# A decoder in one launch: how the second attention hands out VectorE work between its maxima

## The chip, the core and the metric

The kernel runs on one core of one Trainium2 chip. The metric is the device time of one execution in microseconds (us). It is taken as a median of several runs of the same program; beside them one execution is profiled, which gives the rows and the trace that this document quotes. Five engines work from queues of their own: TensorE (PE; its weight loads are listed as PEld), VectorE (DVE), ScalarE (ACT), GpSimd (POOL) and SyncE (SP, which here only issues DMAs). Each engine takes its instructions in the order in which the program emits them, so the order of emission is the schedule.

## The reference

Four residual blocks work on `x` of 4 batches x 512 tokens x 256 features, all in float32:

```python
x = x + L0_xattn(layernorm(x), ctx)   # 8 heads of 4, softmax(q k^T * scale) v, then Wo
x = x + L0_ffn(layernorm(x))          # 8 experts, the best 2 for each token, at most 640 tokens for an expert
x = x + L1_xattn(layernorm(x), ctx)   # 16 heads of 16
x = x + L1_ffn(layernorm(x))          # 15 experts, the best 3 for each token, and a shared expert for all tokens
```

In the last block the router is a softmax over 15 logits for each token; the weights of the three best are normed to a sum of one. An expert computes `fc2(gelu(g) * xh * mult) + b2` with `xh, g = fc1(x) + b1`. The shared expert does the same with twice the width for every token.

## The kernel before

The kernel goes through these stages in order: first attention, the pairs of tiles of the first expert block, second attention, the pairs of tiles of the second expert block, and the sum of the results. Tokens of the expert blocks are written ("put") into a table in DRAM, `xs`, sorted by expert, by indirect DMAs of GpSimd, three for each of the four tiles of 128 tokens in a batch; the experts then read pairs of tiles from it.

**The steps of an attention.** `attention(L, ...)` is a software pipeline written out by hand, counted in steps `t`. A unit is a batch, a group of 8 heads and one half of the group; the second attention has N = 16 units (4 batches, 2 groups, 2 halves) of 8 steps each, so 128 steps. In each step are emitted

- two score products and two row maxima (`maximum`, L669 and L674; VectorE reduces 128x512 scores from PSUM to `negmax`), for the unit that is LEAD = 11 steps ahead,
- two transposed score products and two exponentials (`exponential`, L693 and L698, ScalarE),
- in every other step four products of exponentials and values (`weigh`, L708).

The scores live in a pool of six PSUM banks (`ps_sc`); a step takes four of them, and a bank comes free when its maximum or its exponential has been taken.

**Tasks.** Everything else of the attention with a due time is a task with an earliest and a latest step, given a step of its own by `choose` and `meets`: `helper` (L682, L684, the maxima turned and added to q), `project` (L646 to L661: q or k for a group; two masked copies, one on ScalarE at L659 and one on VectorE at L661, save that k of batches 1 and 2 has both on ScalarE), `values`, `turn`, `rest` (L723 to L739, the division), `turn_back`, `output` (L765, L770).

**Generators.** What has no due time is a generator that yields before each piece of its work. `normalize(b)` adds the results of the first expert block (`combine`, two adds of 128x1024, L1192), takes the mean and variance of the rows (`layer_norm`, L192 to L212), writes the normed rows on ScalarE (L591), and adds the output bias to `x` (L596). It is started 26 steps ahead of the batch's first maximum. `route(f, b, ...)` starts when the second half of the batch's `output` is emitted: again `layer_norm`, four copies of the normed rows into `rows` (L246, ScalarE; one buffer for batches 0 to 2, so batch b+1 has to wait until the puts of batch b have read it), two transposes (L259), logits (L269), some thirty small VectorE instructions for softmax, the best three, counts and places (L280 to L356), the puts (L365, L367) and the transposed weights `combT` (L382, L385). After batch 3 follows `listing` (L401 to L445), which names the pairs that are to be computed.

At the end of each step every living generator runs one piece (two, if it routes batch 1, and two for all once t > 8N). A piece marked TensorE waits for a step without a task.

**The end of the attention.** Two steps after the last unit, `some_shared` begins: one piece a step of the shared expert for batches 0, 1 and 2 in turn, as long as `listing` is not done (`while more[0] < B - 1 and not listed`). What is left of batches 0 to 2 is computed right after the attention, behind the issue of the first three experts' weights and rows (`fetch1`); batch 3's is computed at the very end, and so is what surrounds it:

```python
        for p in range(3):
            fetch1(p)
        for b in more[:-1]:
            for step in (shared_expert, biases):
```

Of the kernel before, what the change touches and what calls it, by code (L numbers as in the profile page):

```python
# [22 lines left out]
P = 128  # L23
# [50 lines left out]
def decoder_kernel(ctx: ExitStack, tc: tile.TileContext, a: dict, out: bass.AP):  # L74
# [106 lines left out]
    V, PEP = "beside", "TensorE"  # L181

    def layer_norm(i, apply, twice=False):
# [4 lines left out]
        for k in range(n):  # L188
            if k % 2 == 0:
                yield V  # L190
# [14 lines left out]
        for step in range(3):  # L205
            if step == 1:
                yield V
# [4 lines left out]
        nc.vector.scalar_tensor_tensor(shift, mv[:, :, 0], -1.0, r, ALU.mult, ALU.mult)  # L212
        for k in range(n):
            yield V
            apply(k, r[:, k : k + 1], shift[:, k : k + 1])
# [24 lines left out]
    def route(f, b, pool, bank):  # L240

        n, K, first = f.n, f.k, f is ffn0
        rows = f.new_rows(b)

        def apply(k, scale, shift):
            nc.scalar.activation(  # L246
# [4 lines left out]
        yield from layer_norm(x[b], apply, twice=first)  # L251
# [3 lines left out]
        for c in range(DC):  # L255
# [4 lines left out]
            if first:  # L260
                scaled(xT[:, c, :], pt, c)
            else:
                (nc.vector.tensor_copy if c == 0 else nc.scalar.copy)(xT[:, c, :], pt)
        logits = pool.tile([P, TB, n], F32, name="logits", tag="logits")
# [34 lines left out]
        )  # L299
        picked = pool.tile([P, TB, n], F32, name="picked", tag="picked")  # L300
        nc.vector.tensor_reduce(picked, chosen.rearrange("p t k e -> p t e k"), AX.X, ALU.add)

        past = pool.tile([P, TB + 1, n], F32, name="past", tag="past", bufs=2)
# [18 lines left out]
        if not first:  # L322
# [6 lines left out]

            by = pool.tile([P, TB, K, n], F32, name="by", tag="by")  # L330
# [30 lines left out]
        for k in range(TB):  # L361
            for _ in range(K):
                yield V
# [14 lines left out]
        if not first:  # L378
# [6 lines left out]
            nc.scalar.copy(combT[:, b * S : (b + 1) * S], pc[: n + 1, :])  # L385
        f.done.add(b)
# [149 lines left out]

    LEAD = 11

    def attention(L, begin, behind, others=None):
# [43 lines left out]
        going = []  # L583

        def normalize(b):
# [7 lines left out]
            yield from layer_norm(x[b], apply)  # L593
            if not shared:
                yield V
                nc.vector.tensor_tensor(x[b], x[b], W["bo"].unsqueeze(1).to_broadcast([P, TB, D]), ALU.add)  # L596
# [7 lines left out]
        def turn(b, c):  # L604
            xn, t = xnT[b]
            pt = ahead([P, S], 0 if b else -LEAD)
# [34 lines left out]
        def project(b, g, n, at=0):  # L641
# [8 lines left out]
            for s in range(2):  # L650
# [7 lines left out]
                elif s == 0 or (n == "k" and 0 < b < B - 1):  # L658
# [126 lines left out]
        def task(lo, hi, f, *needs):  # L785
            tasks.append((lo, hi, f, needs))
# [3 lines left out]
        for n, u in enumerate(units):  # L790
            task(8 * n - 3, 8 * n - 1, lambda u=u: helper(u))
            if not shared or u[2] == 1:
                rests[u] = task(8 * n + 10, 8 * n + (12 if shared and u[0] == 1 else 15), lambda u=u: rest.pop(u)())
        for b in range(B):
            at = 8 * U * b - LEAD
            starts[at - 26] = [lambda b=b: normalize(b)]
# [670 lines left out]
```

## Time and profile before

| | |
|---|---|
| median of 3 runs | 1244.99 us (1244.24 to 1246.53) |
| the profiled execution | 1261.71 us; span of its instructions 1259.7 us, mean granted TensorE clock 0.970 |
| busy: PE, DVE, ACT, POOL | 1183.7, 588.3, 473.2, 192.1 us |
| second attention, first maximum to last exponential | 624.1 to 961.7 us of the span |
| rest of the routing beside the shared expert | to 1024 us |
| shared expert of batch 2, after the attention | 1024.7 to 1047.5 us |
| pairs of the second expert block | from 1048.9 us |

Times inside the span are counted from its start. A line of groups gives the source line, engine, operation, output and input by the program's names with their shapes, the count, the busy time, the mean ns of one, and the idle time of the engine just ahead of them with what ended it. A line of stretches gives, for a stretch of the span, the busy time of PE, PEld, DVE, ACT and POOL (with the number of instructions), the mean granted TensorE clock, the busy share of the DMA engines, and GB/s. The profiled execution is 16.7 us longer than the median of the runs.

### The profile page before, as it was taken

What the parts mean: (1) busy time and instruction counts of PE and PEld (TensorE: products, weight loads), DVE (VectorE), ACT (ScalarE), POOL (GpSimd) and SP (SyncE); (2) the same over time, 40 slices, a digit from 0 to 9 for tenths busy, and PEclk for the clock granted to TensorE, in tenths of its full rate; (3) what the DMA queues carried; (4) which work ended last, traced back from release to release, by engine and by line L of the source; (5) the groups of instructions that cost most, each with busy time, mean ns of one, the idle gap of its engine ahead of it and who ended that gap; (6) DMA issues with size and microseconds to landing.
All of it is one profiled execution on the core that took longest, in us unless ns stands there. A gap on an engine that the chain in (4) does not pass through costs nothing.

```text
span 1259.7 us, 17018 instructions
## 1 busy us (share of the span) xinstructions
PE 1183.7 (94%) x6014; PEld 744.8 (59%) x6014; DVE 588.3 (47%) x1517; ACT 473.2 (38%) x913; POOL 192.1 (15%) x278
## 2 busy tenths in 40 slices
PE   6999997889999999999889999998999999999995
PEld 2333333778888888888523343332334558888873
DVE  7676763431211111111687877866673533222316
ACT  2456454412332222221246565564564312333320
POOL 2000041141001010101200000214003221333330
PEclk9899897999999999999989999999999999999997
DMA  8999115245856565631220100101001043777747
GB/s 289 406 404 403 69 47 227 100 154 185 282 197 213 178 220 173 228 128 56 69 58 1 34 1 1 39 14 51 26 1 38 28 145 102 227 232 225 218 123 241
DMA packets 67393, 183.69 MB, mean 146 GB/s; under 512 B 9934, under 2 KB 32866, under 8 KB 62944
## 3 DMA queue, kind: packets, MB, share of 16 engines
q1 hardware_dynamic: 58944, 161.95, 38.0%
q0 software_dynamic: 8352, 20.53, 4.5%
q8 instruction: 51, 0.84, 0.3%
q14 instruction: 46, 0.38, 0.1%
HBM read 112.08 MB, written 72.74 MB: 147 GB/s over the span
## 4 chain that ended last, share of the span: by engine, by line
PE 39%; DVE 7%; issue 2%; ACT 1%; DMA 1%; POOL 0%; another core or an unknown queue 0%; SPq 0%; POOLq 0%; DVEq 0%; ACTq 0%
PE sc L669 8%; PE av L708 4%; PE pg L1254 4%; PE pv L1254 4%; PE pyp L1310 3%; PE sct L693 3%; DVE negmax L674 2%; PE pp L646 2%; PE shared L1137 2%; PE po L765 1%; PE p L1152 1%; PE p L1137 1%; PE shared L1152 1%; PE ptp L1290 1%; DMA yr<-y 1%
## 5 line engine op out<-in xcount | busy, mean ns | idle before, releaser
L674 DVE TENSOR_REDUCE negmax<-sc 128x1 f32<-128x512 f32 x384 | 245.1, 682 | 72.2 <-PE sct L693 59.0
L698 ACT ACTIVATE es<-sct 128x512 f32<-128x512 f32 x384 | 210.3, 596 | 177.4 <-PE sct L693 159.9
L693 PE MATMUL sct<-qa,kT 32*128 32x512 f32 x768 | 264.3, 657 | 9.7 <-DVE qa L684 4.2
L669 PE MATMUL sc<-kT,qT 32*128 32x512 f32 x768 | 248.3, 646 | 10.8 <-DVE negmax L674 8.3
L669 PEld LDWEIGHTS sc<-kT,qT 32*128 32x128 f32 x768 | 76.9, 185 | 105.3 <-DVE negmax L674 64.8
L958 DVE TENSOR_TENSOR hT<-pu,sg 128x256 f32<-128x256 f32 x112 | 47.6, 425 | 152.7 <-PE pu L950 150.9
L950 PE MATMUL pg<-rT,w 128*128 128x256 f32 x448 | 115.2, 379 | 0.3 <-issue 0.3
L950 PE MATMUL pu<-rT,w 128*128 128x256 f32 x448 | 115.0, 379 | 0.0
L708 PE MATMUL av<-es,v 128*32 128x512 f32 x768 | 108.4, 627 | 0.1
L693 PEld LDWEIGHTS sct<-qa,kT 32*128 32x128 f32 x768 | 80.0, 188 | 40.7 <-issue 16.4
L966 PE MATMUL py<-w,hT 128*128 128x256 f32 x448 | 98.8, 379 | 0.0
L950 PEld LDWEIGHTS pu<-rT,w 128*128 128x128 f32 x448 | 85.1, 190 | 11.6
L966 PEld LDWEIGHTS py<-w,hT 128*128 128x128 f32 x448 | 85.1, 190 | 11.6
L954 ACT ACTIVATE sg<-pg 128x256 f32<-128x256 f32 x112 | 42.8, 382 | 130.3 <-PE pg L950 129.0
L950 PEld LDWEIGHTS pg<-rT,w 128*128 128x128 f32 x448 | 84.0, 190 | 11.6 <-issue 0.5
L1317 POOL DMA_INDIRECT y<-ysb,rows x60 | 59.0, 984 | 144.5 <-ACT ysb L1315 135.1
L364 POOL COPY rows<-weight 128x2 f32<-128x2 f32 (+1 forms) x28 | 4.4, 206 | 464.6 <-DVE weight L328 272.6
L972 POOL DMA_INDIRECT y<-ysb,rows x28 | 27.5, 982 | 269.4 <-ACT ysb L970 269.4
L1260 DVE SCALAR_TENSOR_TENSOR aTp<-pv,wp,gl 128x256 f32<-128x256 f32 x60 | 29.0, 484 | 72.8 <-PE pv L1254 68.9
L1254 PE MATMUL pg<-rTp,wp 128*128 128x256 f32 x240 | 61.8, 380 | 0.3 <-DVE rTp L1294 0.3
L708 PEld LDWEIGHTS av<-es,v 128*32 128x32 f32 x768 | 16.1, 109 | 77.5 <-issue 68.7
L1254 PE MATMUL pv<-rTp,wp 128*128 128x256 f32 x240 | 61.6, 379 | 0.0
(253 smaller groups left out, 1460.5 us busy)
## 6 DMA issues: line engine op xcount, KB each, us to landing
w<-in_W12T_dram SPq DMA_DIRECT2D x17, 2048.0 KB
xs<-empty SPq DMA_DIRECT2D x61, 516.0 KB
w<-in_W3T_dram SPq DMA_DIRECT2D x17, 1024.0 KB
wp<-in_w1p_dram SPq DMA_DIRECT2D x30, 514.0 KB
yr<-y SPq DMA_DIRECT2D x20, 512.0 KB
rows<-xs SPq DMA_DIRECT2D x30, 258.0 KB
wp<-w2s SPq DMA_DIRECT2D x30, 256.0 KB
slots<-empty SPq DMA_DIRECT2D x13, 516.0 KB
```

What stands on the lines that cost most here:

```text
L669: nc.tensor.matmul(sc, q[u][32 * j : 32 * j + 32, qt * P : (qt + 1) * P], k[u][32 * j : 32 * j + 32, :], start=True, stop=True,)
L674: nc.vector.tensor_reduce(heads[:, qt, j, HELP[s] : HELP[s] + 1], sc, AX.X, ALU.max, negate=True)
L693: nc.tensor.matmul(sc, k[u][32 * j : 32 * j + 32, kt * P : (kt + 1) * P], qa[u][32 * j : 32 * j + 32, :], start=True, stop=True,)
L698: nc.scalar.activation(t, sc, AF.Exp, scale=p["scale"])
L708: nc.tensor.matmul(av[b, g][32 * j : 32 * j + 32, :], vs[b % NV][:, kt, h : h + 32], es[u, kt, j], start=(first and kt == 0), stop=(last a ...
L950: nc.tensor.matmul(ph, w[:, c, col : col + P], rT[:, c, :], start=(c == 0), stop=(c == DC - 1))
L954: nc.scalar.activation(sg, pg, AF.Silu)
L958: nc.vector.tensor_tensor(hT0[j][f], pu, sg, ALU.mult)
L966: nc.tensor.matmul(py, hT[f][:, i * P : (i + 1) * P], w[:, f, :], start=(f == 0), stop=(f == NF - 1))
L1137: nc.tensor.matmul(ph, w1[:, c, col : col + P], ffn1.xT[b][:, c, :], start=(c == 0), stop=(c == DC - 1),)
L1254: nc.tensor.matmul(ph[:, :n], w1[:, c, col : col + P], rhs[:, c, :], start=(c == 0), stop=(c == DC - 1),)
L1317: ins = nc.gpsimd.indirect_dma_start(out=y1, out_offset=bass.IndirectOffsetOnAxis(ap=rows[:, i, D : D + 1].bitcast(I32), axis=0), in_=ysb[ ...
```

## The change

The change alters how the generators of the second attention are cut and when a piece may run. The first attention keeps its rule, since `hurry` is always true there.

- **A credit.** Each step adds RATE = 0.9 to a credit that is capped at 1.8. A task takes its `cost` from it (0.7 for `helper`, `rest` and `output` in the second attention, 0 for the others there). A piece marked VectorE or TensorE runs only with a credit of at least COST = 0.6, which it then takes; outside the steps -11 to 8N this does not hold. Pieces marked ScalarE or "little" run without credit, one a step. The doubled pace of batch 1's routing is kept for the first attention alone.
- **Small pieces.** In the second attention the adds of `combine` and of the output bias are halved, `layer_norm` yields ahead of every row tile and every Newton step, and `route` yields at three more places.
- **Norms first.** In a step the generators of `normalize` run ahead of those of `route`; `normalize` starts 34 steps ahead instead of 26.
- **Routing of one batch at a time.** In the second block batch b waits with its copies into `rows`, and with its logits, until batch b-1 is done; batch 3 has buffers of its own and waits with its logits alone. A batch is done two steps after its `combT`.
- **A copy moves.** In the second attention both masked copies of q are made by ScalarE.

```diff
-    V, PEP = "beside", "TensorE"
+    V, ACT, PEP, LITTLE = "VectorE", "ScalarE", "TensorE", "little"
...
+        while not ready():
+            yield LITTLE
         for k in range(n):
-            yield V
+            yield ACT
             apply(k, r[:, k : k + 1], shift[:, k : k + 1])
...
         def apply(k, scale, shift):
+            if k == 0:
+                rows.extend(f.new_rows(b))
...
-        yield from layer_norm(x[b], apply, twice=first)
+        def ready():
+            return first or b == 0 or b - 1 in f.done
+
+        own = not first and b == B - 1
+        yield from layer_norm(x[b], apply, twice=first, fine=not first, ready=lambda: own or ready())
...
+        while not ready():
+            yield LITTLE
         logits = pool.tile([P, TB, n], F32, name="logits", tag="logits")
...
         for k in range(TB):
             for _ in range(K):
-                yield V
+                yield LITTLE
...
             nc.scalar.copy(combT[:, b * S : (b + 1) * S], pc[: n + 1, :])
+
+            for _ in range(2):
+                yield LITTLE
         f.done.add(b)
...
+    RATE, COST = 0.9, 0.6
...
-                elif s == 0 or (n == "k" and 0 < b < B - 1):
+                elif s == 0 or not shared and (n == "q" or 0 < b < B - 1):
...
-            starts[at - 26] = [lambda b=b: normalize(b)]
+            starts[at - (26 if shared else 34)] = [lambda b=b: normalize(b)]
...
+                credit = min(credit + RATE, 2 * RATE)
                 if not free:
-                    steps[t]()
+                    steps[t][0]()
+                    credit -= steps[t][1]
...
-                for w in list(going):
-                    for _ in range(2 if others and (w[2] == 1 or t > 8 * N) else 1):
+
+                for w in sorted(going, key=lambda w: w[2] is not None):
+                    hurry = shared or t > 8 * N or t < -LEAD
+                    for _ in range(2 if others and (shared and w[2] == 1 or t > 8 * N) else 1):
                         if w[1] == PEP:
                             if not free:
                                 break
                             free = False
+                        if w[1] in (V, PEP):
+                            if credit < COST and not hurry:
+                                break
+                            credit -= COST
...
             for yr in yrs:
-                yield V
-                nc.vector.tensor_tensor(x[b], x[b], yr, ALU.add)
+                for i in range(0, TB, 2):
+                    yield V
+                    xs = x[b][:, i : i + 2, :]
+                    nc.vector.tensor_tensor(xs, xs, yr[:, i : i + 2, :], ALU.add)
```

## The prediction

> **What bounds the kernel now.** I read the page's slices first, then the groups, then the second attention as a timeline of VectorE, then the stretches and the chain around its end.
>
> ```profile
> PE   6999997889999999999889999998999999999995
> DVE  7676763431211111111687877866673533222316
> ```
>
> TensorE is busy nearly everywhere; VectorE is full only in the two attentions (slices 1 to 6 and 20 to 29). The costliest group there is the row maxima:
>
> ```profile
> L674 DVE TENSOR_REDUCE negmax<-sc 128x1 f32<-128x512 f32 x384 | 245.1, 682 | 72.2 <-PE sct L693 59.0
> ```
>
> Pairs of maxima number the steps: the second attention's first pair, at 624.13 us, is t = -11. In quiet steps VectorE waits for TensorE; where other work is emitted between the pairs, TensorE waits for a score bank that the maximum has not freed. The timeline of VectorE, t = 8 and 9, then 71 to 73:
>
> ```profile
> 664.41 1.29 DVE L674 TENSOR_REDUCE negmax<-sc 128x1 f32<-128x512 f32 x2 [0.88 <-PE sct L693]
> 666.07 1.29 DVE L674 TENSOR_REDUCE negmax<-sc 128x1 f32<-128x512 f32 x2 [0.37 <-PE sct L693]
> ...
> 814.43 1.29 DVE L674 TENSOR_REDUCE negmax<-sc 128x1 f32<-128x512 f32 x2 [0.36 <-PE sct L693]
> 817.37 0.69 DVE L770 TENSOR_TENSOR x<-po,x 128x512 f32<-128x512 f32 x1 [1.65 <-PE po L765]
> ...
> 820.11 1.25 DVE L674 TENSOR_REDUCE negmax<-sc 128x1 f32<-128x512 f32 x2
> ...
> 823.80 1.28 DVE L674 TENSOR_REDUCE negmax<-sc 128x1 f32<-128x512 f32 x2
> ```
>
> The reader should see the brackets of idle time vanish, and steps of 5.7 and 3.7 us in place of about 2. Soon after, ScalarE is held by DMA: batch 1's copies into `rows` wait for batch 0's puts, with exponentials queued behind them. Its timeline:
>
> ```profile
> 827.49 1.95 ACT L246 ACTIVATE rows<-x,shift,r 128x768 f32<-128x768 f32 x2 [1.57 <-DMA xs<-rows,put]
> ```
>
> The end of the attention is TensorE's. Stretches, the chain of waits, and SyncE's timeline:
>
> ```profile
> 872.00:888.00 16.00, 11.34 (x52) 3.92 (x46) 4.65 (x7) 3.81 (x7) 6.11 (x10) 0.68 0.16 58
> ...
> 964.00:1024.00 60.00, 56.95 (x220) 35.34 (x218) 27.81 (x106) 15.53 (x21) 22.83 (x30) 1.00 0.16 53
> 1028.00:1032.00 4.00, 4.00 (x10) 1.71 (x9) 0.84 (x2) 0.69 (x1) 0.00 (x0) 1.00 1.05 387
> 1032.00:1034.00 2.00, 2.00 (x6) 0.95 (x5) 0.66 (x1) 0.45 (x1) 0.00 (x0) 1.00 0.48 154
> ```
>
> ```profile
> 1022.89 1.73 DVE x L1164 x4
> 1024.67 14.00 PE p L1137 x32
> 1038.67 6.91 PE p L1152 x32
> 1045.57 1.92 PE p L1163 x8
> 1047.49 0.60 PE ptp L1290 x4
> ```
>
> ```profile
> 1022.37 0.33 SPq L1116 DMA_DIRECT2D wp<-in_w1p_dram  x1
> ...
> 1025.24 2.41 SPq L1281 DMA_DIRECT2D rows<-xs  x4
> ```
>
> SyncE's first weight load for the second expert block is issued at 1022.37, once the last product of the looped shared experts has let go of its memory. The rows follow six weight loads, and the DMA engines are full until about 1033. Nobody feels it: batch 2's shared expert (1024.67 to 1047.49) runs meanwhile.
>
> **Which base.** The profiled execution took 1261.71 us (span 1259.7 and 2.0 around it), 16.7 more than the median of 1244.99. I set the sum against the profiled steps, leave one stall out, and apply the difference to the median. The stall is t = 91 to 93 (872.49 to 888.22, 15.7 us where three steps take 5.9): TensorE stops and resumes at half clock. It ends when a dozen puts in a row end, and I can't name its cause; it fits the 16.7 us, so I take it to be the profile's own.
>
> **Where the routing goes.** 32 steps earn 28.8 of credit; their ten tasks of 0.7 (four `helper`, four `rest`, two `output`) leave 21.8, or 36 pieces of 0.6. One batch needs 14 paid pieces of `normalize` and 23 of `route`: 37. So nothing catches up, and one-at-a-time queues it. Laying the pieces on the steps one after the other by the rule: `normalize` of batches 1, 2, 3 runs at t = -13 to 4, 19 to 36, 51 to 70 (before: -5 to 5, 27 to 37, 59 to 69). Batch 0 is routed at t = 91 (before 73); batch 1 copies rows at 92 and is done at 136 (before 91); batch 2 at 153 (135); batch 3 at 166 (150). The listing ends at 169 (153). The shared expert takes 14 pieces a batch, from 130, 144, 158. Before, the listing came ahead of 158 and two batches ran in the loop; now three do.
>
> **Sum, part by part.**
>
> Steps 4 to 111 (656.50 to 932.28). A quiet step is 1.98 us (t = 4 to 15 take 23.75). A 2 us product (q or k projection, output, logits; 16 of them both before and after) adds 1.5, by a fit over 20 windows of four steps. Above that, before loses: t = 27 to 32, 2.9; 37 to 42, 3.2; 51 to 64, 6.4; 69 to 72, 4.3; 73 to 75 (the wait for puts), 4.0; 79 to 82, 3.0; 108 to 111, 1.8. Together 25.6. After, VectorE has 1.21 for the maxima and at most 0.9, in my count 0.82 over t = 51 to 82, for the rest: 2.03 to 2.11, against 1.98. Over the 60 steps in which the credit is used up (19 to 30, 39 to 46, 51 to 82, 104 to 111) that is 3 to 8. `rows` copies (four of 1.02 us, L246) and q's copies (now 1.56 of ScalarE where 0.78 and VectorE's 0.81 were) come in the same steps at t = 48: 1 to 2 more. I leave 10 and gain 15.
>
> Halving an add costs 0.16 us (1216 ns for 1024 columns, 688 for 512, L1192 and L770), 2 us of VectorE for twelve, inside the 0.82. If VectorE's slack were gone it would be paid in full. q's copies hold ScalarE instead of VectorE; behind them wait exponentials instead of maxima, so I cost the move at nothing, with 2.5 either way in the range. Norms first only swaps pieces within a step, in the first attention too: nothing, 0.5 either way. The waits for a done batch are in emission: nothing queues behind them, and POOL's copies and three puts of 1.27 us a tile simply come later, nine steps per batch instead of six or fewer, slower than POOL's 15 us. SyncE's `yr` loads go out eight steps earlier, with nothing due behind them.
>
> The start, t = -11 to 3 (32.4 us): VectorE was full from -5 to 0 (17.1 us); with batch 1's norms begun at -13 that is some 13, and the idle steps ahead grow by 1: minus 2.5. Ahead of it, value copies no longer split batch 0's norms (0.7 at 615): minus 0.5.
>
> Steps 112 to 129: one of batch 2's transposes and its logits leave (2.5 of TensorE): minus 2.
>
> The loop after 8N. TensorE gains batch 1's `combT` (1.0), batch 2's transposes (1.3), logits (1.9) and ranks (0.8): 5. There is no idle time to hide it (56.95 of 60 busy). Another 0.5 for VectorE's bursts, since both remaining routings run hurried. Softmax of batch 2 now falls between gelus, two table loads more of 1.28 us each; ScalarE is busy 15.5 of 60 us, so nothing by the row. The Trainium skill ("ScalarE: Activation LUTs", "What ACT_TABLE_LOAD costs") adds a drain, 2.66 us per switch: 5.3 if nothing covered it, which would cancel the whole gain. The 8 us of ScalarE idle ahead of the existing gelu load decides for the row.
>
> The handover. Batch 2's shared expert costs TensorE the same inside the loop, but no longer covers the loads. Issue 1022.37; rows 0 are the seventh of ten transfers, through at about 76% of the bytes, 1031; the biases end at 1024. Idle: 7. Then the clock: in the 872 to 888 row it was halved from 876.7 to 886.9, five us past the restart at 881.9, so 2.5 lost. The skill ("TensorE: Matmul & The Clock Gate", Part 1) says that an idle window of about 3.4 us halves the clock and as long a busy one restores it: 1.7 lost, a sum 0.8 lower. I take 2.5. This rule speaks against the change, as before never idles here.
>
> Sum: -15 - 2.5 - 0.5 - 2 + 5.5 + 7 + 2.5 = -5. From 1244.99: **1240**.
>
> **Rivals.**
> *The handover outweighs the smoothing.* A straight-line fit of the same windows charges 0.37 us per us of VectorE work wherever it lies. Then pieces save only the 12.6 us of VectorE work that leaves t = 4 to 111 (4.7), and the two waits at 71 to 75 (6): 11, with 3 at the start and 2 at the end 16; the loop and handover take 15, and 4 to 5 more if the last puts, now issued until t = 165, land after the last product. About 1249. It decides where the steps up to 129 save under 15. For it: the fit itself. Against: t = 53 to 58 held 6.7 us of pieces and took 13.9, just VectorE's own busy time.
> *The stall at 872 is in every run* and ends with the burst of puts, which three-step spacing removes: another 10 off, 1230. For it: it ends with the burst. Against: 16.7 us of profile excess.
> *The credit changes little*: gain and loss cancel within 2.5 us; 1245.
>
> **Chances.** Forecast 0.45; handover outweighs 0.20; stall in all runs 0.20; cancel 0.15. 0.2% (2.5 us) is what a measurement of this kernel can tell from no change. The forecast and the stall are faster: 0.65; the cancelling case is same, 0.15; slower 0.20. The range reaches into both outer cases, 1226 to 1252; the forecast's own is 1233 to 1242.
>
> **What would show it.** After: pairs of maxima 2.0 to 2.2 us apart from t = 19 to 111, the last exponentials some 20 us nearer to the first maximum (30 if the stall is missing), the shared expert's products three batches long ahead of the weight loads, no L1137 between the loads and the first L1290, and TensorE idle some 7 us there at half clock after. I am wrong if two batches remain in the loop, if rows land before the biases end, or if ScalarE takes VectorE's place as what frees the banks.

## The result, and the profile after

The changed kernel takes 1235.13 us (median of 6 runs, 1230.71 to 1237.14); the kernel before, on the same chip, 1245.24 (6 runs, 1244.02 to 1249.63). The ratio is 0.9907, 95% interval 0.9888 to 0.9927: a gain of 10.1 us where 5 were forecast. The profiled execution of the changed kernel took 1236.06 us, span 1234.0, mean granted clock 0.972.

The two rows of slices, and the group of the maxima (count and busy time, then the idle time ahead of them):

```profile
PE   6999997899999999999889999999999979999995
DVE  7677763541112111121587887886754432222216
```

```profile
L697 DVE TENSOR_REDUCE negmax<-sc 128x1 f32<-128x512 f32 x384 | 245.6, 683 | 70.6 <-PE sct L716 66.0 <-PE sc L692 4.2
```

VectorE's second full part is denser and over a slice sooner (the drop to 5 and less begins in slice 30), and TensorE has a new 7 in slice 33. The timeline of VectorE, the quiet steps t = 8 and 9, then t = 71 (797.09) to 74 (805.22):

```profile
654.35 1.29 DVE L697 TENSOR_REDUCE negmax<-sc 128x1 f32<-128x512 f32 x2 [0.88 <-PE sct L716]
656.01 1.29 DVE L697 TENSOR_REDUCE negmax<-sc 128x1 f32<-128x512 f32 x2 [0.37 <-PE sct L716]
...
797.09 1.28 DVE L697 TENSOR_REDUCE negmax<-sc 128x1 f32<-128x512 f32 x2
799.88 0.69 DVE L793 TENSOR_TENSOR x<-po,x 128x512 f32<-128x512 f32 x1 [1.50 <-PE po L788]
800.93 1.29 DVE L697 TENSOR_REDUCE negmax<-sc 128x1 f32<-128x512 f32 x2 [0.36 <-PE sct L716]
...
803.38 1.25 DVE L697 TENSOR_REDUCE negmax<-sc 128x1 f32<-128x512 f32 x2
...
805.22 1.28 DVE L697 TENSOR_REDUCE negmax<-sc 128x1 f32<-128x512 f32 x2
```

The quiet steps are what they were. The output's step is still long (3.8 us: VectorE waits 1.50 for the product itself), the next two take 2.5 and 1.8. The pairs t = 4 and t = 112 bound the main stage, first in the changed kernel (250.1 us apart), then in the kernel before (269.6 us, run `before_third` below):

```profile
646.43 1.29 DVE L697 TENSOR_REDUCE negmax<-sc 128x1 f32<-128x512 f32 x2 [1.36 <-PE sct L716]
896.53 1.29 DVE L697 TENSOR_REDUCE negmax<-sc 128x1 f32<-128x512 f32 x2
```

```profile
647.50 1.89 DVE L674 TENSOR_REDUCE negmax<-sc 128x1 f32<-128x512 f32 x3 [1.36 <-PE sct L693]
917.09 1.88 DVE L674 TENSOR_REDUCE negmax<-sc 128x1 f32<-128x512 f32 x3
```

ScalarE's copies into `rows` no longer wait for a DMA, and alternate with the exponentials (batch 1, t = 92 on):

```profile
846.70 1.09 ACT L721 ACTIVATE es<-sct 128x512 f32<-128x512 f32 x2 [1.15 <-PE sct L716]
847.67 1.03 ACT L250 ACTIVATE rows<-x,shift,r 128x768 f32<-128x768 f32 x1
848.59 1.08 ACT L721 ACTIVATE es<-sct 128x512 f32<-128x512 f32 x2
```

At the end of the attention, stretches (busy time of PE, PEld, DVE, ACT, POOL, then clock, DMA share, GB/s): the loop with three batches of the shared expert, the idle handover, and the first products after it. Then the chain of waits there:

```profile
925.00:1010.80 85.80, 83.95 (x329) 52.52 (x326) 39.88 (x156) 26.02 (x34) 28.91 (x44) 1.00 0.13 45
1011.00:1019.00 8.00, 0.00 (x1) 0.03 (x1) 0.22 (x1) 0.00 (x0) 0.00 (x0) 0.54 1.02 351
1019.00:1026.00 7.00, 6.92 (x21) 5.59 (x22) 1.87 (x3) 0.47 (x1) 0.00 (x0) 0.55 0.18 58
```

```profile
1006.91 1.94 PE shared L1187 x8
1011.74 7.13 DMA rows<-xs
1019.00 1.10 PE ptp L1327 x4
```

TensorE does nothing from 1010.75 to 1019.00 while the DMA engines are full, and the clock is at half from 1011.7 to 1025.3. SyncE issues the first weight load at 1008.97 and the rows at 1011.74, as the last looped products end.

### The profile page after: what moved, and what is told of

Same layout as the page of the kernel before. It is cut to its first block, busy times and chain, and to the rows that moved or that the text cites. A ratio compares the mean times of both kernels' runs of the same rounds, so it can differ in the third digit from the quotient of the medians.

```text
span 1234.0 us, 17009 instructions
## 1 busy us (share of the span) xinstructions
PE 1168.3 (95%) x6014; PEld 743.5 (60%) x6014; DVE 580.7 (47%) x1521; ACT 479.4 (39%) x923; POOL 189.7 (15%) x278
## 4 chain that ended last, share of the span: by engine, by line
PE 44%; DVE 3%; DMA 3%; issue 1%; ACT 1%; SPq 0%; POOL 0%; POOLq 0%; DVEq 0%; ACTq 0%
PE sc L692 10%; PE av L731 5%; PE pg L1291 4%; PE pv L1291 4%; PE pyp L1347 3%; PE shared L1172 3%; PE sct L716 2%; PE pp L669 2%; PE shared L1187 1%; PE po L788 1%; PE pa L641 1%; PE ptp L1327 1%; DVE negmax L697 1%; DMA rows<-xs 1%; DMA y<-ysb,rows 1%
## 5 line engine op out<-in xcount | busy, mean ns | idle before, releaser
L716 PE MATMUL sct<-qa,kT 32*128 32x512 f32 x768 | 253.0, 648 | 5.0 <-DVE qa L707 3.0
L692 PE MATMUL sc<-kT,qT 32*128 32x512 f32 x768 | 245.1, 648 | 3.7 <-DVE negmax L697 1.9
L731 PE MATMUL av<-es,v 128*32 128x512 f32 x768 | 105.5, 609 | 0.6 <-ACT es L721 0.6
L716 PEld LDWEIGHTS sct<-qa,kT 32*128 32x128 f32 x768 | 79.7, 186 | 29.4 <-issue 15.7
L1007 POOL DMA_INDIRECT y<-ysb,rows x28 | 27.5, 982 | 269.4 <-ACT ysb L1005 269.4
```

The costliest lines, as they stand in the source:

```text
L692: nc.tensor.matmul(sc, q[u][32 * j : 32 * j + 32, qt * P : (qt + 1) * P], k[u][32 * j : 32 * j + 32, :], start=True, stop=True,)
L716: nc.tensor.matmul(sc, k[u][32 * j : 32 * j + 32, kt * P : (kt + 1) * P], qa[u][32 * j : 32 * j + 32, :], start=True, stop=True,)
L731: nc.tensor.matmul(av[b, g][32 * j : 32 * j + 32, :], vs[b % NV][:, kt, h : h + 32], es[u, kt, j], start=(first and kt == 0), stop=(last a ...
```

## Which executions can be compared

The 25.6 us between the two first profiles were not the gain. Later runs came from four chips, and these fall into two groups: on chips 4 and 15 the kernel before takes 1245 us as in the first comparison (group A), on chips 8 and 9 it takes 1264 to 1265 (group B). Each chip was used on one occasion only, so the record cannot tell the chip from the occasion. The first profile of the kernel before (1261.71) has group B's stage times, that of the changed kernel group A's. The stages of two executions of each kernel and group, in us (t counted by pairs of maxima):

| | before, A | before, B | changed, A | changed, B |
|---|---|---|---|---|
| to the first maximum of the second attention | 615.8 | 630.3 | 616.0 | 623.9 |
| t = -11 to 3 | 31.7 | 31.7 | 30.4 | 27.6 |
| t = 4 to 111 | 269.6 | 276.0 | 250.1 | 250.1 |
| t = 112 to the first shared product | 31.7 | 31.7 | 28.5 | 29.6 |
| shared expert of batches 0 to 2 | 86.8 | 83.4 | 85.7 | 97.7 |
| idle to the first pair | 0 | 0 | 8.25 | 6.55 |
| from there to the end of the span | 214.4 | 212.0 | 215.0 | 213.4 |

The columns are `before_third`, `before_again`, the changed kernel's first profile and `after_again`. The execution of `before_third` was itself 6.6 us over its chip's median: by longer stretches of half clock it loses 2.8 us at t = 72 to 75 and 3.4 in the shared expert against the other profiles of this kernel.

The largest difference between the groups lies ahead of the second attention, in work that the change hardly touches: the first attention took 181 to 186 us in the nine profiles with group A's times and 186 to 193 in the nine with group B's, while the pairs of the first expert block took 295.7 us in all of them.

**The kernel before, unchanged** (`before_again` on chip 8, one execution: 1267.06, and `before_third` on chip 15: 1251.97, where the median was 1245.35).

> The kernel before, unchanged, for a second profiled execution. Theory 1 (the stall at t = 91 to 93 belongs to that one profiled execution): steps 91 to 93 take about 6 us, t = 4 to 111 take 266 (275.8 before, less 9.8), the profiled span is about 1243 us, and the difference to the changed kernel's span of 1234.0 is 9 to 12. Theory 2 (the stall is in every execution of the kernel before and the burst of puts makes it): steps 91 to 93 take 14 us or more again with TensorE at half clock after, and t = 4 to 111 take about 276; then the changed kernel's gain there is 25.7, not 15.9, and something else must have cost it 15. Also wanted: the time from the first attention's last exponential to the second attention's first maximum, and the loop of the shared expert (83.4 before), from an undisturbed profile.

> The kernel before, unchanged, for another look. Where its time is near 1264, theory 1 (the freeze at the end of batch 1's twelve puts is part of this kernel's time there) expects 15.2 to 15.3 us for the four steps from t = 88 again, and theory 2 (it comes and goes) expects 9 in some execution. Where its time is near 1245, theory 1 expects the freeze to be missing, 9 to 10 us for these steps and 266 for t = 4 to 111; theory 2 that it is there and the 19 us between the two times lie elsewhere.

The four steps from t = 88 took 15.27 us on chip 8 and 8.77 on chip 15. VectorE and then ScalarE in `before_again`:

```profile
880.85 0.69 DVE L674 TENSOR_REDUCE negmax<-sc 128x1 f32<-128x512 f32 x1 [2.14 <-PE sc L669]
886.65 1.89 DVE L674 TENSOR_REDUCE negmax<-sc 128x1 f32<-128x512 f32 x3 [5.12 <-remote]
```

```profile
881.56 0.60 ACT L698 ACTIVATE es<-sct 128x512 f32<-128x512 f32 x1 [1.47 <-PE sct L693]
886.61 0.57 ACT L385 COPY combT<-bank 16x512 f32<-16x512 f32 x1 [4.46 <-remote]
```

and ScalarE at the same place in `before_third`:

```profile
865.43 1.08 ACT L698 ACTIVATE es<-sct 128x512 f32<-128x512 f32 x2 [0.63 <-PE sct L693]
867.44 0.57 ACT L385 COPY combT<-bank 16x512 f32<-16x512 f32 x1 [0.92 <-PE bank L382]
```

On group B VectorE and ScalarE stop for 5 us around the last of batch 1's twelve puts (869.6 to 884.6), TensorE with them, and the two go on within 0.1 us of each other; "remote" says that the trace names no releaser. All three were idle at once for 2.5 us. On group A the same copy waits 0.92 us for TensorE. So the stall that the prediction left out is no accident of one execution: it is in both profiles of this kernel with group B's times, and in that of `before_three` below. It is absent in `before_third`, on the group where 1245 is measured. A like stop stands in the first attention of `before_again` (VectorE and ScalarE idle and TensorE busy for 0.02 us from 196.70 to 200.10, during the first block's puts), and none in the profiles of group A.

**The changed kernel, again** (`after_again` on chip 9, `after_third` on chip 4).

> The changed kernel, unchanged, beside the kernel before. Where the kernel before takes 1264 (with the stall of t = 88 to 91 in its profile) in place of 1245, theory 1 (the stall belongs to the kernel before on such a chip and the change removes it, the rest of the difference between the chips is common to both kernels) expects 1243 to 1246, 19 to 21 below the kernel before, with t = 4 to 111 at 250.1 again. Theory 2 (the chip adds the same to both) expects 1253 to 1255, 10 below. Where the kernel before takes 1245, both expect 1235.

> The changed kernel, unchanged, as the yardstick for the other runs of this call. Two kinds of chip have been seen: on the one the kernel before takes 1245 and its t = 88 to 91 take 8.8 us; on the other 1264 and 15.3. Theory 1 (the gain is the same on both kinds, since each kernel has its own freezes on the second kind): 9 to 12 below the kernel before. Theory 2 (it depends on the kind): 9 to 12 below on the first kind, and outside 5 to 14 below on the second.

On chip 9: 1255.38 against 1265.04, ratio 0.9919 (0.9892 to 0.9947), with t = 4 to 111 at 250.05. On chip 4: 1236.25 against 1245.53, 0.9924 (0.9895 to 0.9952). The gain is 9 to 10 us on both groups. On group B the changed kernel does not have the stall at t = 88, but it has its own, in the loop (97.7 us where group A takes 85.7: TensorE's three longest gaps are 4.3, 2.0 and 1.2 us, and the rest is half clock). The longest comes again at the end of puts in a row:

```profile
1016.43 0.40 DVE L434 TENSOR_TENSOR shared<-earlier,shared 128x225 f32<-128x225 f32 x1
1019.47 0.42 DVE L1191 TENSOR_TENSOR x<-shared,x 128x256 f32<-128x256 f32 x1 [2.64 <-remote]
```

**One word of the kernel before** (`before_single`, chip 9):

```diff
-                    for _ in range(2 if others and (w[2] == 1 or t > 8 * N) else 1):
+                    for _ in range(2 if others and (shared and w[2] == 1 or t > 8 * N) else 1):
```

> The kernel before, with one thing altered: the routing of batch 1 no longer runs two pieces a step in the second attention (it keeps that in the first). Its twelve puts then come three at a time, some steps apart, in place of twelve in 15 us. Theory 1 (the stall of all engines at t = 88 to 91 comes with twelve puts in a row): the stall is gone, the four steps from t = 88 take 9 in place of 15.2, and with the doubled pace t = 79 to 82 lose 2 less: 8 to 12 below the kernel before where that shows the stall, 1 to 3 below where it doesn't. Theory 2 (the stall belongs to the place in the program, or to the chip): it stays at the copy of the transposed weights, wherever that has moved, and the gain is 1 to 3. In both, batch 1 is done about 12 steps later and batch 2's copies into rows may wait for its puts, 1 to 3 us of loss.

1254.13 against 1265.04, ratio 0.9903 (0.9869 to 0.9938). The puts of batch 1 now come in threes over 27.5 us, the four steps from t = 88 take 9.44, and t = 4 to 111 take 260.43 in place of 275.95. Only 5.8 of these 15.5 us are the four steps of the stop. Another 8.0 were gained at t = 69 to 80, ahead of it, where the routing of batch 1 begins and now runs one piece a step. Part of the gain came back: the shared expert took 89.1 in place of 83.4, with all engines idle for 1.2 us at the end of batch 3's twelve puts in a row and two stretches of half clock. Theory 1 holds for the stop; ahead of it, it expected a gain of 2. On group B this one edit, a part of the change, gains as much as the whole change. It was not run on group A.

## What made the steps shorter

**No credit** (`no_credit`, chip 8): `RATE, COST = 5.0, 0.6`.

> The changed kernel with RATE = 5.0 in place of 0.9, so that the credit never holds a piece back: small pieces, norms first, one batch at a time and the moved copy stay. By the tally of the order of emission the batches are done at t = 81, 117, 143, 156 and the listing ends at 159 (91, 136, 153, 166 and 169 with the credit); three batches stay in the loop, so the handover is unchanged. Theory 1 (pace is the gain: VectorE work that falls on few steps is paid in full, since a step has 0.8 us to spare): t = 4 to 111 take 258 to 266 in place of 250.1, the loop 2 to 4 less, total 1240 to 1247. Theory 2 (what counts is how much work lies ahead of t = 111 and how small the pieces are, the credit itself is worth nothing): t = 4 to 111 within 5 us of 250.1, total 1233 to 1238.

1265.68 us, ratio to the kernel before 1.0007 (0.9983 to 1.003): the whole gain is gone on this group. But not in the steps: t = 4 to 111 took 250.97, so there the credit is worth 0.9 us, as theory 2 said. Theory 1 had the right total for a wrong reason. What was lost lies after t = 112. Batch 2's copies into `rows` now fall at t = 118 (136 with the credit), among the last exponentials, when there are no maxima left and TensorE needs each exponential at once. ScalarE, then two stretches:

```profile
917.18 1.03 ACT L250 ACTIVATE rows<-x,shift,r 128x768 f32<-128x768 f32 x1
918.10 1.08 ACT L721 ACTIVATE es<-sct 128x512 f32<-128x512 f32 x2
```

```profile
914.50:925.50 11.00, 9.40 (x60) 2.82 (x56) 1.40 (x4) 10.13 (x18) 0.85 (x5) 1.00 0.04 13
925.50:942.50 17.00, 17.00 (x67) 7.52 (x62) 2.27 (x16) 5.71 (x12) 0.00 (x0) 0.50 0.00 1
```

ScalarE is busy 10.13 of 11 us, TensorE 9.40; then the clock is at 0.50 for 17 us. From the last maximum to the last exponential it takes 28.0 us; the changed kernel takes 16.6. The loop took 99.2, of which group B's freezes are a part (5.9 us ahead of batch 2's `combT`).

**No credit and pieces as large as before** (`coarse`, one execution on chip 15, 1240.86 us; `coarse_timed`, chip 4). The edit takes back `fine`, the halved adds and the three new yields; the cut shows a part of it:

```diff
-    RATE, COST = 0.9, 0.6
+    RATE, COST = 5.0, 0.6
...
-            yield from layer_norm(x[b], apply, fine=not shared)
+            yield from layer_norm(x[b], apply, fine=False)
...
-                for i in range(0, TB, 2):
-                    yield V
-                    xs = x[b][:, i : i + 2, :]
-                    nc.vector.tensor_tensor(xs, xs, yr[:, i : i + 2, :], ALU.add)
+                yield V
+                nc.vector.tensor_tensor(x[b], x[b], yr, ALU.add)
```

> The changed kernel without credit (RATE = 5.0) and with the pieces as large as before: adds of 128x1024, two row tiles of statistics a piece, Newton steps in two pieces, three fewer places to yield in the routing. Norms first, the start 34 steps ahead, one batch at a time and the copies of q on ScalarE stay. Wanted is the time of t = 4 to 111: 275.95 before, 260.43 before with batch 1 at single pace, 250.97 without credit but with small pieces. Theory 1 (small pieces are what smooths: no step gets more than 0.6 us more than its maxima and one task): 257 to 261. Theory 2 (the order does it: no doubled pace, norms and routing apart in time, q's copies): 250 to 253.

> The changed kernel without credit and with pieces as large as before, now timed. In its one look t = 4 to 111 took 263.8 (250.1 changed, 269.6 before), two batches were in the loop, there was no idle handover. Theory 1 (small pieces gain 13 us in the steps, and lengthen the routing so that the handover of 11 us opens; the two nearly cancel): 1235 to 1240 where the kernel before takes 1245, 0 to 5 above the changed kernel. Theory 2 (the handover and the loop cost the changed kernel less than 8): 6 or more above the changed kernel.

t = 4 to 111 took 263.84 and 263.72: against 250.97 without credit the large pieces cost 12.8 us there. In both profiles 10.2 us of these steps run at half clock, which costs up to 5.1 of the 12.8; in the changed kernel none do. The timeline of VectorE at t = 52 (759.21):

```profile
756.39 1.22 DVE L1220 TENSOR_TENSOR x<-x,yr 128x1024 f32<-128x1024 f32 x1
758.16 0.22 DVE L286 COPY logits<-bank 128x60 f32<-128x60 f32 x1 [0.55 <-PE bank L279]
759.21 1.29 DVE L690 TENSOR_REDUCE negmax<-sc 128x1 f32<-128x512 f32 x2 [0.83 <-PE sct L709]
760.42 1.22 DVE L1220 TENSOR_TENSOR x<-x,yr 128x1024 f32<-128x1024 f32 x1
```

Each generator runs one piece a step, so the size of a piece already limits what a step gets, and the credit adds little to small pieces. At 1.22 us for an add beside 1.29 for the pair of maxima and a task, a step is over 1.98. Large pieces with the credit were not run. And 12.8 is not a share of the gain that adds up with others: `before_single` has large pieces too, and reaches 260.43 with one altered word. The timed total was 1242.59 against 1236.25 for the changed kernel on that chip and 1245.53 before (ratio to before 0.9973, 0.9960 to 0.9986). So small pieces and the credit together are worth 6.3 us net, just past the line to theory 2: 13.6 in the steps and 3.2 at t = 112 to 129, less 2.6 in the shared expert (85.7 against 83.1) and 8.2 of idle handover, which the large pieces do not have: with fewer pieces the listing comes ahead of the third looped batch, and batch 2's shared expert covers the loads.

**q's copy back on VectorE** (`q_back`, chip 15, one execution: 1241.28 us):

```diff
-                elif s == 0 or not shared and (n == "q" or 0 < b < B - 1):
+                elif s == 0 or (n == "k" and 0 < b < B - 1):
```

> The changed kernel with q's second masked copy back on VectorE, eight copies of 0.81 us in the second attention, six of them in t = 4 to 111. Wanted is the time of t = 4 to 111, 250.05 with the copies on ScalarE. Theory 1 (VectorE is full in those steps and each copy is paid there): 253 to 255. Theory 2 (the copy on ScalarE is paid as well, by exponentials that come later): 249.5 to 251, and the move is worth nothing.

t = 4 to 111 took 250.60 against 250.09. The move is worth 0.5 us: theory 2.

**A higher rate with spaced puts** (`rate12_spaced`, chip 15):

```diff
-    RATE, COST = 0.9, 0.6
+    RATE, COST = 1.2, 0.6
...
-                    for _ in range(2 if others and (shared and w[2] == 1 or t > 8 * N) else 1):
+                    for again in range(2 if others and (shared and w[2] == 1 or t > 8 * N) else 1):
+                        if again and w[1] == LITTLE and not shared:
+                            break
```

> The changed kernel with RATE = 1.2, and after step 8N pieces marked LITTLE run one a step in place of two, so that the twelve puts of batches 2 and 3 come three at a time, two to three steps apart. By the tally batch 2 is done at 149, batch 3 at 169, the listing ends at 171, and three batches stay in the loop (to 172). Its twin with the same early schedule and puts in a row is the run without credit (loop from the first shared product to the last 99.2 us, total 1265.7). Theory 1 (twelve puts in a row freeze all engines at their end and halve the clock after): the loop takes 86 to 91 us, total 1253 to 1258. Theory 2 (the loop is long for another reason: the doubled pace, or ScalarE): 96 to 100 us again, total 1263 to 1267.

1244.68, ratio 0.9979 (0.9960 to 0.9999). The loop took 83.4 us. That tells nothing between the theories: this is a chip of group A, where puts in a row freeze nothing in any profile. What it does show is the loss after t = 112 once more, on this group too: 29.9 us from the last maximum to the last exponential, with the clock at half for 20.5. The half clock does not come in every execution: `rate12_two` below emits the same up to there, and kept the full clock (21.2 us). Its stretch:

```profile
915.00:925.00 10.00, 8.39 (x52) 3.02 (x52) 1.38 (x3) 8.45 (x15) 0.00 (x0) 1.00 0.01 2
```

## What the handover costs

**Three batches in the loop of the kernel before** (`before_three`, chip 9): `while more[0] < B - 1:`.

> The kernel before with three batches of the shared expert in the loop whatever the listing says, so that nothing is left between the issue of the first weights and the pairs. Theory 1 (the handover's price, idle TensorE and half clock after it, comes from the third batch in the loop alone): TensorE idle 7 to 9 us ahead of the first turned pair and 2.5 to 3.5 us at half clock after: 10 to 12 above the kernel before. Theory 2 (it is the late routing, puts that end at 1006 us shortly before the loads, that holds the first rows back): the rows are there early, since the puts end some 20 us ahead of the loads; idle under 4 us, 3 to 5 above.

1275.27 against 1265.04, ratio 1.0072 (1.0050 to 1.0095): 9.1 us dearer (6.3 to 12.0). The idle stretch and the one after it:

```profile
1055.00:1063.70 8.70, 0.03 (x1) 0.01 (x1) 0.49 (x2) 0.00 (x0) 0.00 (x0) 0.52 1.01 341
1063.70:1071.00 7.30, 7.28 (x26) 6.01 (x27) 1.87 (x3) 0.95 (x2) 0.00 (x0) 0.64 0.13 41
```

8.7 us idle with the DMA engines full, then half clock, although the last put had ended at 1024.7, 30 us earlier. The third looped batch alone makes the gap; late routing is not needed for it.

**Two batches in the loop of the changed kernel** (`two_in_loop`, chip 8): `while more[0] < B - 2 and not listed:`.

> The changed kernel, but only batches 0 and 1 have their shared expert in the loop after step 8N; batch 2's is computed behind the issue of the first weights and rows again, as before. Theory 1 (the late routing is what the handover pays for, the listing ends at t = 169 and the two looped batches end at 158): the idle 8.25 us at the handover and the 3 us of half clock after it vanish (11 off), but from t = 158 to 169 TensorE has little but batch 3's routing, whose VectorE pieces and puts take 8 to 10 us: a new wait of 7 to 10 us takes its place, total 1232 to 1236, not to be told from the changed kernel by more than 3. Theory 2 (the handover is the price of the third looped batch alone, and batch 3's routing is short when hurried two pieces a step): 1224 to 1227, TensorE idle under 3 us between the loop and the first product of batch 2's shared expert.

1250.84 against 1264.04, ratio 0.9896 (0.9864 to 0.9928); the changed kernel on the other chip of group B had 0.9919. The intervals overlap, so no gain over it is shown: theory 1. TensorE between the loop and batch 2's shared expert (1008.98):

```profile
1001.91 1.89 PE L397 MATMUL bank<-ident,comb 128*16 128x128 f32 x8 [3.08 <-DVE place L365]
1004.46 0.61 PE L419 MATMUL bank<-past,ones 128*128 128x15 f32 x2 [0.66 <-ACT combT L400]
1008.28 0.41 PE L460 MATMUL bank<-ident,shared 128*1 128x23 f32 x4 [3.22 <-DVE shared L453]
1008.98 8.58 PE L1172 MATMUL p<-xT,ctxT 128*128 128x512 f32 x14 [0.29 <-issue]
```

The gap has moved: TensorE now waits for batch 3's routing, at half clock for 17.1 us.

**Two batches and RATE 1.2** (`rate12_two`, chip 8): both edits together.

> The changed kernel with RATE = 1.2 in place of 0.9 and two batches in the loop in place of three. By the tally the listing ends at t = 159, as the second looped batch ends at 158, so that batch 2's shared expert again covers the loads at the handover. Theory 1 (the gain is the pace, the loss is the handover, and they are separate): t = 4 to 111 lose 3 to 8 against the changed kernel (a step then may hold 1.2 us of other VectorE work beside 1.21 of maxima, 0.4 over the 1.98 of a quiet step), the handover gives back 11 and the loop 2: total 1224 to 1231. Theory 2 (the pace at 0.9 is what matters, at 1.2 the steps are as full as without credit): the gain of t = 4 to 111 shrinks by 10 or more, total 1234 to 1240.

1255.02 (1245.01 to 1264.51), ratio 0.9924 (0.9903 to 0.9944). Taken to 1245 that is 1235.7, the total of theory 2, but not for its reason: t = 4 to 111 took 250.27, so the rate costs nothing there; 21.2 us went from the last maximum to the last exponential, and 5.2 and 7.8 us passed ahead of batch 2's and 3's `combT`.

**Late biases** (`late_bias`, chip 9, and `late_bias_again`, chip 4): the eight small products of `biases`, 1.9 us a batch, move from the loop to behind the issue of the loads.

```diff
-                while b not in ffn1.done:
-                    yield V
-                yield from biases(b, new)
...
-        for b in more[:-1]:
-            for step in (shared_expert, biases):
+        for b in range(B - 1):
+            for step in (shared_expert, biases) if b in more else (biases,):
```

> The changed kernel, with the products of the routing weights and the second biases (biases, 1.92 us of TensorE for each batch) of batches 0 to 2 moved out of the loop to behind the issue of the first weights and rows. By the tally three batches then take 36 steps from 130 on and end at 166, the listing at 169. Theory 1 (what is moved behind the issue fills the idle time one for one): the loop shortens by 4 to 6, the idle 8.25 us at the handover shrink by 5.8, less half clock: 3 to 7 below the changed kernel. Theory 2 (the loop then waits for the listing, whose steps without a product are as long as before, and the loads start no earlier against the routing): the gain is lost again, within 2.5 of the changed kernel.

> The changed kernel with the products of routing weights and second biases of batches 0 to 2 behind the issue of the first weights and rows, again, now beside the changed kernel on one chip. Theory 1 (work behind the issue fills the idle time one for one): 4 to 7 below the changed kernel. Theory 2 (the first loads wait for batch 3's puts, which end no earlier, so only what the loop had too much is saved): 1 to 4 below.

On group B 1248.44 (0.9860, 0.9826 to 0.9895) beside 1255.38 for the changed kernel, theory 1's size: TensorE goes from the biases to the first pair without the 6.55 us of idle time. On group A 1235.33 beside 1236.25, no difference that can be measured. TensorE in `late_bias_again`:

```profile
1002.02 0.29 PE L419 MATMUL bank<-past,ones 128*128 128x15 f32 x2
1005.51 0.38 PE L460 MATMUL bank<-ident,shared 128*1 128x23 f32 x4 [3.20 <-DVE shared L453]
1006.18 9.33 PE L1198 MATMUL p<-fc2b,combT 16*128 16x256 f32 x24 [0.29 <-DVE list L463]
1019.82 1.94 PE L1324 MATMUL ptp<-ident,rows 128*128 128x128 f32 x8 [4.31 <-DMA rows<-xs]
```

The loop's last product ended at 1002.19, but SyncE issued the first weight load only at 1009.37, 2.0 us after the last of batch 3's puts had ended on GpSimd. Two things hold the loads: the last looped product, and the puts. SyncE's waits say so, first in the changed kernel, then in `late_bias_again` (total, count, longest):

```profile
SPq L1151 <- DMA xs<-yr,put: 150.2, 1, 150.2
SPq L1151 <- PE shared L1187: 0.9, 1, 0.9
```

```profile
SPq L1151 <- DMA xs<-yr,put: 152.3, 1, 152.3
```

In the changed kernel both end within a microsecond (the product comes 0.9 us after the put has landed, the first load at 1008.97), so moving one of them alone gains nothing on this group: theory 2.

**Late biases, RATE 1.2, and batch 2 held back** (`hold_late`, chip 4): the puts come earlier too, and batch 2's copies stay out of the last exponentials.

```diff
-            return first or b == 0 or b - 1 in f.done
+            return first or b == 0 or b - 1 in f.done and (b != B - 2 or len(norms) > 0)
```

> The kernel with the late biases, RATE = 1.2, and batch 2's copies into rows held back until the loop of the shared expert begins (t = 130). By the tally batch 2 is done at 150, batch 3 at 163, and the listing ends at 166, as the third looped batch does (153, 166, 169 in the changed kernel). Theory 1 (the loss at higher rates lies in batch 2's copies into rows among the last exponentials, t = 115 to 125, where TensorE goes to half clock for 17 to 20 us, and not in the steps up to 111): first to last exponential as in the changed kernel within 2 us, half clock there gone, the handover 3 us earlier than with the late biases alone: 6 to 10 below the changed kernel. Theory 2 (a higher rate costs in the steps themselves): 2 or more above the kernel with the late biases alone.

1228.39 (1226.14 to 1229.71), ratio to the kernel before 0.9852 (0.9823 to 0.9880), 7.9 below the changed kernel on the same chip. Stretches, the loop and the handover:

```profile
923.70:999.70 76.00, 75.64 (x292) 47.50 (x290) 35.14 (x138) 25.40 (x33) 25.54 (x36) 1.00 0.12 42
999.70:1010.80 11.10, 8.38 (x28) 6.11 (x28) 6.08 (x19) 0.00 (x0) 0.00 (x0) 0.67 0.84 287
```

TensorE has only 0.4 us idle in the loop and 2.7 in the handover. t = 4 to 111 took 250.26 and the last exponentials 16.0: theory 1. This version beats both kernels on this chip; it was not run on group B.

## Why the prediction was right or wrong

The direction and the range held; the size did not: -5 forecast, -10 measured. Term by term, on group A. The first column is the recorded sum; the second compares the changed kernel's first profile with `before_third`, less the 6.2 us of half clock named above.

| term | forecast | measured |
|---|---|---|
| ahead of the second attention | -0.5 | +0.2 |
| t = -11 to 3 | -2.5 | -1.3 |
| t = 4 to 111 | -15 | -16.7 |
| t = 112 to 129 | -2 | -3.2 |
| loop | +5.5 | +2.3 |
| idle handover | +7 | +8.25 |
| half clock after it | +2.5 | +0.6 (whole rest of the span) |
| sum | -5 | -9.85 |

**The loop is the term that was mis-sized most.** The step that failed reads "There is no idle time to hide it (56.95 of 60 busy)". The 3 us that the row leaves free were there to be filled. For the same work, the shared expert of three batches, the first profile of before shows

```profile
964.00:1047.50 83.50, 79.93 (x293) 48.90 (x292) 34.36 (x118) 18.28 (x25) 22.83 (x30) 1.00 0.22 78
```

and the changed kernel's row above 83.95 of 85.80. TensorE's own work grew by 4.0, not 5, and its idle time fell from 3.57 to 1.85. The half microsecond for VectorE's bursts did not show. Together that is the 3.2 by which the term was too high, two thirds of the 4.85 between the two sums.

The table loads came as counted, five in the loop where there were three, and cost nothing that shows; the 5.3 reckoned for loads with their drain did not appear in the loop's time. ScalarE at the first of the two new ones goes from its copies to the exponential of the softmax in 1.7 us, 1.28 of them the load, and the rest a wait for VectorE:

```profile
949.29 1.95 ACT L250 ACTIVATE yr<-x,shift,r 128x768 f32<-128x768 f32 x2
951.25 1.28 ACT L293 ACT_TABLE_LOAD   x1
952.98 0.25 ACT L293 ACTIVATE ex<-ex 128x60 f32<-128x60 f32 x1 [0.45 <-DVE ex L292]
```

**Routing times.** The tally of steps held in kind: batch 1 copies `rows` at t = 92, three batches run in the loop, no product of `p` stands between the loads and the first pair. The first rows landed 10.0 us after the first load's issue, where 8.6 were reckoned: hence 8.25 idle, not 7. The half clock lasted 6.3 us past the restart at 1019.00, which costs 3.2; 2.5 was taken from the trace of before, and 1.7 from the rule of the Trainium skill ("TensorE: Matmul & The Clock Gate", Part 1). In the other profiles with a gap of 6.5 us or more it lasted 4.4 to 6.1, so 2.2 to 3.2 are lost in all: 2.5 stands inside, 1.7 below every one.

**What one execution can't settle.** The last row of the table says 0.6 only because `before_third` is long there (214.4). The other profiles in which batch 2's shared expert or the biases fill the gap took 211.8 to 212.7 from the first pair to the end, on both groups; those with a gap of 6.5 us or more took 213.4 to 215.5. So this term was about right. The row of t = -11 to 3 depends on the execution too: the first profile has 6.8 us of half clock there, `after_third` has none and takes 27.65, which makes the row -4.0. The steps, t = 112 to 129 and the loop repeat within 0.1 us in `after_third` (250.08, 28.52, 85.71).

**The steps.** -16.7 against -15 is near, but the reason given, at most 0.9 of other work a step by the credit, is not what did it: without credit the steps take 0.9 us more. The size of the pieces (12.8, without credit) and the end of the doubled pace (15.5 by itself on group B, the stop included) are what the runs show. q's copies, costed at nothing with 2.5 either way, are worth 0.5. Pairs of maxima were 2.36 us apart on the average from t = 19 to 111, not 2.0 to 2.2, the products of projections and outputs included.

**The base.** Leaving the stall at t = 91 to 93 out was right for the chips that gave 1244.99, though "the profile's own" was the wrong name: it belongs to a group of chips. That the 15.7 us fit the 16.7 was luck: the first profile also reached the second attention 8.3 us later than `before_third` (624.1 against 615.8), and 9.8 us off for the stall would have left it 6.9 above the median. On that group the rival "the stall is in every run" describes the kernel before, and its 1230 does not follow, because the changed kernel has freezes of its own, 12 us in the loop.

**The rivals.** "The handover outweighs the smoothing" was to win where the steps up to 129 save under 15; they saved 21. The loop and the handover took 11 of it back by the table. "The credit changes little" is true of the credit in the steps, and false of the change.

## What to carry to other kernels

Where every generator runs one piece a step, look first at the size of the pieces and at whatever runs two of them; here a budget was worth 0.9 us for smoothing, and on group B the whole gain for the place in time at which work falls. When a profile's time is not the median of the timed runs, ask whether both come from the same chip before naming the difference. A gap that several things hold open (here the last product and the last put) closes only when all of them move.

## What the hardware showed that was not expected

- Two groups of two chips each differ by 19 us for one kernel (1245 and 1264 to 1265). On one of them TensorE, VectorE and ScalarE are all idle for up to 3.9 us at once during or at the end of some, not all, runs of puts 1.27 us apart; with the puts in threes some steps apart (`before_single`) the stop at t = 88 was absent. Why they stop was not settled.
- Where TensorE was busy 9.40 of 11 us, waiting in small gaps (the longest 1.6 us) for ScalarE, the granted clock fell to 0.50 for 17 us, in the run without credit. A long idle stretch was not needed for it. With gaps as long, `rate12_two` kept a clock of 1.00, so the busy share alone does not decide it.
- In all 18 profiles each stretch at half clock, but for the last of each profile, lasted a whole multiple of 3.41 us (3.4, 6.8, 10.2, 13.7 and so on up to 23.9). So the same wait can cost more or less: after gaps of 8.2 us in the changed kernel the clock came back 5.5 us past the restart in `after_third`, 6.3 in the first profile.
